# A hand-written order for attention with shared keys and values: a new sequence of steps, input loads one cycle earlier, and centred rows in PSUM at the end

## The chip, the cores and the metric

The kernel runs on one core of a Trainium2 chip. The metric is the device time of one execution in microseconds (us), lower is better. All arithmetic is float32. The engines are named as in the profile: PE multiplies matrices (PEld is its weight load), DVE, ACT and POOL work on vectors, SP issues the transfers (DMAs).

## What is computed

For 64 batches of x (128 tokens by 512), with 16 heads of size 64 that share one key and one value per token, the reference is:

```python
xn = layernorm(x, g_in)
q = (xn @ Wq).reshape(b, n, 16, 64).transpose(0, 2, 1, 3) * 64 ** -0.5
k, v = split(xn @ Wkv)                       # one head, shared by all 16
k = concat([null_k, k]); v = concat([null_v, v])   # one extra key ahead
sim = einsum('bhid,bjd->bhij', q, k) + bias  # bias of head, query, key
sim = where(causal_mask, -max, sim); sim = where(mask, sim, -max)
out = einsum('bhij,bjd->bhid', softmax(sim), v)
out = out.transpose(0, 2, 1, 3).reshape(b, n, 1024) @ Wo
return x + layernorm(out, g_out)
```

## The kernel before

**Tiling.** Batches are handled in pairs, and tokens in groups of four batches (GB = 4). The query product of a group is done by Strassen's scheme with sums of token blocks (xS1 to xS4, made on POOL at L492) and of weight blocks (wS): `q_one(c, k, h)` with k from 1 to 8 gives the products, named q1 to q8 below (a stroke, q1', marks the second half h = 1 of a cycle). A product is four matmuls (L597) of 256 columns into PSUM tiles pa, pc or pw. Three of the seven products are split once more, into leaves: `leaf(c, k, stage)`, called leaf(k,stage) here, multiplies sums of smaller blocks (xL2, xL3, xL4, made on POOL at L534, with one block of xT overwritten) at L553 into pl, and DVE adds the result to the query tile at L556. ACT copies pa out at L503 and L614 (L608 keeps a part, ku), DVE adds pc at L1001 and L1009 and L617.

The output product works likewise: `out_one(p, k)` (out1 to out7, eight matmuls each, L860), with sums of the attended values on POOL at L843 (`out_sum`), parts kept by ACT at L893 and added by DVE at L885.

**Softmax.** For each batch there are scores (PE, L651), added to bias and mask by DVE (L687), row maxima (DVE, L692), exps with row sums (ACT, L701), reciprocals (DVE, L718), the scaling by them (POOL, L722), a transpose of 32 by 32 blocks (DVE, L737), and the values (PE, L770). ACT evicts the values from PSUM at L810. The tile of bias plus mask is made on POOL (L635).

**Layer norms.** x is loaded (SP, L128, four DMAs per batch after the first groups), its statistics are taken on DVE (L284 to L288), the power on POOL (L289), and it is normed on ACT (L310), transposed in blocks on DVE (L331), written to DRAM (xd, L340) and read back as tokens (xT, L348). Keys and values come from xT (PE pkv, L358; DVE, L373); values go through DRAM too (vd, L387; vr, L399), keys are copied at L393. The output row y gets its statistics on DVE (L909 to L913), the power on POOL (L917), is normed on ACT (L932), multiplied by the gain (L953), added to the residual (L956) and stored (L960). The last batches do this on DVE alone: `pair_center` (L942) subtracts the mean and multiplies by the gain, `pair_scale` (L948) multiplies by the reciprocal deviation and adds the residual.

**Order.** No scheduler moves anything: each engine runs its instructions in the order in which the code emits them. The program is a front (a list of calls, with regions -1 and 0), then `cycle(c)` for c = 1 to 29, then a final list for the last six batches. Cycle c holds, for b0 = 2c and b1 = b0 + 1: the softmax of b0 and b1; the output product of p = b0 - 2 and p + 1; the output norm of r = b0 - 4 and r + 1; the norm of x for m = b0 + 10 and m + 1; the query products for b0 + 4. It ends with `region(c)`: the scores of b0 + 2 and b0 + 3 and the values of b0 and b0 + 1, which share the weights' half arrays. Even cycles begin a token group and so hold its POOL sums; odd cycles hold the tokens' read back. What sets the time of a step is thus its place in its engine's queue and the semaphores that it waits for; SP waits too, so a transfer stands behind the waits of those issued ahead of it. PSUM tiles come from small pools: pl, pw, pkv and pyw share two slots, pa and pc have one each, and the score tiles ("s") have one pool of their own. `nc.tensor.addr_align` pads PE's instructions so that a block of 256 begins at a chosen place.

Of the kernel before, what the change touches and what calls it, by code (L numbers as in the profile page):

```python
# [17 lines left out]
def kernel(  # L18
# [67 lines left out]
    GB = 4  # L86
# [847 lines left out]
    gain = [gob]  # L934

# [4 lines left out]
    def pair_center(b):  # L940
        mv, rstd = yn[b]
        nc.vector.scalar_tensor_tensor(  # L942
            ys[b], ys[b], mv[:, 0:1], gain[0], ALU.subtract, ALU.mult
        )

    def pair_scale(b):
        mv, rstd = yn.pop(b)
        nc.vector.scalar_tensor_tensor(  # L948
            ys[b], ys[b], rstd, res.pop(b), ALU.mult, ALU.add
        )  # L950
# [120 lines left out]
    def cycle(c):  # L1071
# [5 lines left out]
        fetch, send = (b0 + 5) // GB, (b0 + 7) // GB  # L1077
        if soft:
            scores_max(b1, 0)
        if first and LEAF <= c and more:  # L1080
            token_sum(c // 2 + 1, 1)
        if pair:
            values_out(p, (0, 2))
        if first and LEAF <= c and more:
            token_sum(c // 2 + 1, 3)
        if fin:
            pair_stats(r)
        if first and LEAF <= c and more:
            token_sum(c // 2 + 1, 2)
        if pair:  # L1090
            values_out(p + 1, (0, 2))
        if not first and fetch + 1 < NG:
            load_mask(fetch + 1)
        if m < B:
            load_x(m)
        if fin:
            pair_pow(r)
        if c == 1:
            tokens_in(2)
        if soft:  # L1100
            scores_max(b1, 1)
            scores_max(b0, 0)
        q_one(c, 1, 0)
        if fin:
            pair_stats(r + 1)
        if pair:
            values_out(p, (1, 3))
        if first and LEAF <= c and more:
            token_sum(c // 2 + 1, 4)
        if pair:  # L1110
            values_out(p + 1, (1, 3))
        if first and LEAF <= c and more:
            leaf_sums(c // 2 + 1, 2)
        if c < LEAF:
            q_one(c, 2, 0)
        if soft:
            exps(b0, 0, 0, 2)
            scores_max(b0, 1)
        if c >= LEAF:
            leaf(c, 2, 0)  # L1120
        q_one(c, 5, 0)
        q_one(c, 6, 0)
        if first and LEAF <= c and more:
            leaf_sums(c // 2 + 1, 3)
        if soft:
            exps(b0, 0, 2, 8)
        if pair:
            out_sum(p, 0)
        if first and LEAF <= c and more:
            leaf_sums(c // 2 + 1, 4)  # L1130
        out_one(p, 1)
        if pair:
            out_sum(p, 1)
        if fin:
            pair_pow(r + 1)
        if soft:
            rinv(b0, 0)
        q_one(c, 7, 0)
        if m + 1 < B:
            load_x(m + 1)  # L1140
        if c % 2 and n0 < B:
# [493 lines left out]
```

## Time and profile before

| quantity | value |
|---|---|
| median of 3 runs (lowest to highest) | 1035.18 us (1034.01 to 1036.33) |
| the profiled execution's own time | 1035.38 us |
| its span in the trace | 1033.6 us |
| granted PE clock | 0.997 |
| share of the span busy: PE, DVE, ACT, POOL | 98%, 84%, 62%, 76% |

A row of a timeline gives start, duration, engine, line, operation, output and input names, shapes and count, and in brackets how long the engine stood before it and what ended that. Durations of neighbouring rows overlap a little, since instructions are pipelined: the time from one start to the next says what a step costs its engine. A product of four matmuls takes PE 0.87 us from start to start, one of eight 1.73.

### The profile page before, as it was taken

The numbers are of one execution on the slowest core, as the hardware profiler recorded it, in microseconds if no ns is written. First come the engines' busy times: TensorE is split into PE (matmuls) and PEld (weight loads), VectorE is DVE, ScalarE is ACT, GpSimd is POOL, SyncE is SP. The second block draws the span as 40 slices with busy tenths as digits, with TensorE's granted clock in tenths as the row PEclk, the third lists the DMA queues.
The fourth block names the chain that finished last, engine by engine and source line by source line (L and its number), as shares of the span: only waits on it lengthen the run. The fifth ranks groups of instructions, "written<-read, shape, count | busy, mean of one in ns | idle before, by whom it ended". The sixth has DMA issues, their size and how long they took to land. (4 is left out here: it accounts for less than half of the span.)

```text
span 1033.6 us, 31778 instructions
## 1 busy us (share of the span) xinstructions
PE 1017.9 (98%) x12104; PEld 894.1 (87%) x12104; DVE 864.3 (84%) x2000; ACT 644.0 (62%) x2742; POOL 787.5 (76%) x710
## 2 busy tenths in 40 slices
PE   9999999999999999999999999999999999999996
PEld 8878888889888888888889888888888898888875
DVE  7766888888888898888888888888888988878898
ACT  2655776556775656766557765557756567755581
POOL 3699959588696877959679595886968779596774
PEclk9999999999999999999999999999999999999998
DMA  6541160522506144151521605225051431502202
GB/s 210 164 131 48 73 156 23 149 82 88 151 33 151 59 126 114 72 131 39 147 93 72 167 21 147 75 94 145 32 155 55 129 111 72 126 13 63 83 2 102
DMA packets 70263, 100.90 MB, mean 98 GB/s; under 512 B 27744, under 2 KB 31328, under 8 KB 68320
## 3 DMA queue, kind: packets, MB, share of 16 engines
q1 hardware_dynamic: 69008, 97.83, 33.3%
q8 instruction: 96, 1.57, 0.7%
q10 hardware_dynamic: 1104, 1.05, 0.3%
q14 instruction: 55, 0.45, 0.1%
HBM read 63.19 MB, written 33.55 MB: 94 GB/s over the span
## 5 line engine op out<-in xcount | busy, mean ns | idle before, releaser
L701 ACT ACTIVATE s<-s,nmax 128x65 f32<-128x65 f32 (+1 forms) x1024 | 377.0, 400 | 3.4 <-DVE nmax L692 3.4
L722 POOL TENSOR_TENSOR s<-s,rinv 128x1024 f32<-128x1024 f32 (+1 forms) x128 | 188.5, 1483 | 57.1 <-DVE rinv L718 56.6
L701 ACT ACTIVATION_READ_ACCUMULATOR s<-s,nmax 128x1 f32 x1024 | 229.2, 224 | 0.0
L635 POOL TENSOR_TENSOR s<-biasp,mneg 128x1552 f32<-128x1552 f32 x64 | 205.0, 3225 | 2.3 <-DMA x<-in_x_dram 2.0
L810 ACT ACTIVATE oT<-poX,nv 128x256 f32<-128x256 f32 x58 | 27.6, 476 | 219.8 <-PE poX L770 112.7
L556 DVE TENSOR_TENSOR qT<-pl,qT 128x128 f32<-128x128 f32 (+1 forms) x420 | 128.6, 329 | 9.5 <-PE pl L553 6.9
L687 DVE TENSOR_TENSOR s<-ps,s 128x256 f32<-128x256 f32 (+2 forms) x224 | 120.1, 604 | 15.7 <-PE ps L651 15.2
L860 PE MATMUL pyX<-wo,oT 128*128 128x256 f32 x512 | 121.5, 380 | 0.0
L692 DVE TENSOR_REDUCE nmax<-s 128x8 f32<-128x520 f32 (+1 forms) x128 | 118.8, 949 | 0.1
L860 PE MATMUL pyX<-wT,oT 128*128 128x256 f32 x488 | 115.5, 380 | 0.8 <-POOL oT L843 0.8
L737 DVE STREAM_TRANSPOSE sb<-s 128x1536 f32<-128x1536 f32 x64 | 112.9, 1764 | 0.2 <-POOL s L722 0.2
L860 PEld LDWEIGHTS pyX<-wo,oT 128*128 128x128 f32 x512 | 96.9, 190 | 14.6 <-issue 0.9
L860 PEld LDWEIGHTS pyX<-wT,oT 128*128 128x128 f32 x488 | 88.4, 190 | 10.8 <-POOL oT L843 1.2
L651 PE MATMUL ps<-kT,qT 64*64 64x128 f32 (+1 forms) x4096 | 93.6, 245 | 1.0 <-issue 1.0
L917 POOL TENSOR_TENSOR rstdo<-rstdo,nhalf 128x1 f32<-128x1 f32 x64 | 35.5, 557 | 75.6 <-PE pl L553 68.3
L651 PEld LDWEIGHTS ps<-kT,qT 64*64 64x64 f32 x4096 | 85.5, 134 | 6.0 <-issue 2.6
L289 POOL TENSOR_TENSOR rstd<-rstd,nhalf 128x1 f32<-128x1 f32 x64 | 37.3, 583 | 65.2 <-DVE rstd L288 59.2
L770 PE MATMUL pos<-sb,vr 32*64 32x128 f32 (+1 forms) x1792 | 81.8, 321 | 0.0
L770 PE MATMUL poY<-sb,vr 32*64 32x128 f32 x720 | 74.8, 347 | 0.2 <-issue 0.2
L770 PE MATMUL poX<-sb,vr 32*64 32x128 f32 x960 | 73.7, 299 | 0.0
L503 ACT COPY qT<-pa 128x256 f32<-128x256 f32 x168 | 66.7, 397 | 1.4 <-PE pa L597 1.4
L860 PE MATMUL pyw<-wo,oT 128*128 128x256 f32 x280 | 66.4, 380 | 0.3 <-POOL oT L843 0.2
(150 smaller groups left out, 2514.8 us busy)
## 6 DMA issues: line engine op xcount, KB each, us to landing
res<-in_x_dram SPq DMA_DIRECT2D x64, 256.0 KB, 3.0
out_dram<-y SPq DMA_DIRECT2D x58, 256.0 KB, 2.0
x<-in_x_dram SPq DMA_DIRECT2D x224, 64.0 KB, 2.7
xd<-xb SPq DMA_DIRECT2D x14, 1024.0 KB, 3.9
xT<-xd SPq DMA_DIRECT2D x56, 256.0 KB, 5.9
vr<-vd SPq DMA_DIRECT2D x64, 128.0 KB, 2.7
x<-in_x_dram SPq DMA_DIRECT2D x8, 256.0 KB, 4.9
vd<-vt SPq DMA_DIRECT2D x32, 64.0 KB, 2.2
```

The costliest lines, as they stand in the source:

```text
L289: nc.gpsimd.tensor_tensor(rstd, rstd, nhalf, ALU.pow)
L503: nc.scalar.copy(q_part(g, c, h), by_block("a"))
L556: nc.vector.tensor_tensor(o, p, o, ALU.add)
L635: nc.gpsimd.tensor_tensor(S[b], biasp, mneg[:, t].unsqueeze(1).broadcast_to([P, R8, ROW]), ALU.add,)
L651: nc.tensor.matmul(to[r][i * DH : (i + 1) * DH, f, :], qT[g, f // FH, t // GH][rows, f % FH, t % GH, NQ - 1 - i if hf else i], kT[g][rows, ...
L687: nc.vector.tensor_tensor(sv, ps, sv, ALU.add)
L692: nc.vector.tensor_reduce(nmax[b][:, hf], S[b][:, :, WITH_NULL[hf]], AX.X, ALU.max, negate=True)
L701: nc.scalar.activation(row, row, AF.Exp, bias=nmax[b][:, hf, k : k + 1], accum_out=rsum[b][:, hf, k : k + 1],)
L722: nc.gpsimd.tensor_tensor(sv, sv, rinvs.pop((b, hf)).unsqueeze(2).broadcast_to([P, R8, sv.shape[2]]), ALU.mult,)
L737: nc.vector.transpose(sb.rearrange("p j e q -> p e j q"), S[b][:, :, 1 : ROW - 1].rearrange("p e (j k) -> p e j k", k=Q),)
L770: nc.tensor.matmul(po[s][rows, half], vr[g][quad(s), j, t, :], sb[quad(s), slots, r * NF : (r + 1) * NF, :], start=start, stop=True, skip_ ...
L860: nc.tensor.matmul(prod[key], h[:, c, :], w[:, c, :], start=(start and c == 0), stop=(c == HC - 1), skip_group_check=not start,)
```

## The change

The work is the same but for one thing: in the last six batches `pair_center` writes the centred row to a PSUM tile, and `pair_scale` reads it there. All else is order:

- In `cycle`, nearly every call has a new place. q5 comes ahead of the leaf and of q6; q5' comes in the middle of the second half, right behind out6; leaf(2,3) and leaf(4,0) come earlier, q8' later. In cycle 1 (whose groups have no leaves) out2 stands between q7 and q4. The first norm of r has its statistics ahead of the maxima, xL3 and the first output sum come ahead of xS4 and xL2 on POOL.
- x is loaded a cycle ahead: cycle c loads m + 2 and m + 3, each behind a store, in place of m and m + 1 (cycle 1 loads all four).
- The front and the final list have new sequences.

The core of the diff:

```diff
@@ pair_center, pair_scale
+    y_mid = {}
     def pair_center(b):
         mv, rstd = yn[b]
+        if b < B - 6:
+            o = ys[b]
+        else:
+            if b // 2 not in yns:
+                yns[b // 2] = ps_s.tile([P, 2, DIM], FP, tag="s", name=f"yc_{b}")
+            o = y_mid[b] = yns[b // 2][:, b % 2]
         nc.vector.scalar_tensor_tensor(
-            ys[b], ys[b], mv[:, 0:1], gain[0], ALU.subtract, ALU.mult
+            o, ys[b], mv[:, 0:1], gain[0], ALU.subtract, ALU.mult
         )
     def pair_scale(b):
         mv, rstd = yn.pop(b)
         nc.vector.scalar_tensor_tensor(
-            ys[b], ys[b], rstd, res.pop(b), ALU.mult, ALU.add
+            ys[b], y_mid.pop(b, ys[b]), rstd, res.pop(b), ALU.mult, ALU.add
         )
@@ cycle
-        if m < B:
-            load_x(m)
...
-        if m + 1 < B:
-            load_x(m + 1)
...
+        if c == 1:
+            load_x(m)
...
+        if c == 1:
+            load_x(m + 1)
...
+        if m + 2 < B:
+            load_x(m + 2)
+        if soft:
+            nc.tensor.addr_align(256, offset={1: 120, B // 2 - 3: 76}.get(c, 94))
...
-        if soft:
-            nc.tensor.addr_align(256, offset={B // 2 - 3: 141}.get(c, 159))
...
+        if m + 3 < B:
+            load_x(m + 3)
+        if pair:
+            load_res(p + 1)
...
@@ front
-    q_one(0, 4, 0)
...
+    q_one(0, 4, 0)
+    q_one(0, 3, 0)
+    key_values(6)
+    q_one(0, 1, 1)
+    q_one(0, 2, 1)
+    q_half(2, 1)
...
@@ final list
     pair_center(B - 5)
     out_sum(B - 2, 1)
     out_sum(B - 2, 3)
+    pair_scale(B - 5)
     pair_pow(B - 3)
-    pair_center(B - 3)
     pair_scale(B - 6)
     store(B - 6)
-    pair_scale(B - 3)
-    store(B - 3)
-    pair_scale(B - 5)
+    out_one(B - 2, 5)
     store(B - 5)
     pair_pow(B - 4)
+    pair_center(B - 3)
+    pair_scale(B - 3)
     out_sum(B - 2, 2)
     pair_center(B - 4)
-    out_one(B - 2, 5)
+    stats_part(B - 2, 0)
     pair_scale(B - 4)
     store(B - 4)
     out_one(B - 2, 6)
     out_one(B - 2, 3)
-    stats_part(B - 2, 0)
     stats_part(B - 2, 1)
+    store(B - 3)
```

How the rows move on the engines:

**SP and POOL in the steady cycle.** SP's transfers from the end of an even cycle through the odd one behind it (x are the input rows, xd and xT the tokens, vd and vr the values, out_dram the stores), before:

```order
L340 DMA xd_7_4913<-xb_7_4433 128x2048
L387 DMA vd_6_4924<-vt_6_4922 512x1x32 x2
L348 DMA xT_7_4927<-xd_7_4913 32x4x512 x4
L138 DMA res_19_4934<-in_x_dram 128x512
L393 DMA kT_6_4389<-kT_6_4389 64x512
L145 DMA m8_7_5088<-in_mask_BxS_bk0_dram 128x512
L128 DMA x_32_5090<-in_x_dram 32x512 x4
L128 DMA x_33_5151<-in_x_dram 32x512 x4
L399 DMA vr_6_5193<-vd_6_4924 32x1024 x4
L960 DMA out_0_dram<-y_18_4753 128x512
L960 DMA out_0_dram<-y_19_4890 128x512
```

and now:

```order
L340 DMA xd_7_4932<-xb_7_4412 128x2048
L348 DMA xT_7_4936<-xd_7_4932 32x4x512 x4
L138 DMA res_18_4941<-in_x_dram 128x512
L387 DMA vd_6_4945<-vt_6_4943 512x1x32 x2
L393 DMA kT_6_4388<-kT_6_4388 64x512
L145 DMA m8_7_5084<-in_mask_BxS_bk0_dram 128x512
L399 DMA vr_6_5212<-vd_6_4945 32x1024 x4
L967 DMA out_0_dram<-y_18_4754 128x512
L128 DMA x_34_5264<-in_x_dram 32x512 x4
L967 DMA out_0_dram<-y_19_4892 128x512
L128 DMA x_35_5331<-in_x_dram 32x512 x4
```

The loads of x moved from ahead of vr to behind the two stores, and are those of the next cycle (34 and 35 for 32 and 33); vd moved behind xT. On POOL, the even cycle's sums before:

```order
L492 TENSOR_TENSOR xS4_7_5522<-xT_7_4927,xS2_7_5494 128x512
L534 TENSOR_TENSOR xL2_7_5526<-xT_7_4927 128x128 x2
L534 TENSOR_TENSOR xL2_7_5526<-xT_7_4927,xL2_7_5526 128x128
L534 TENSOR_TENSOR xT_7_4927<-xT_7_4927,xL2_7_5526 128x128
L534 TENSOR_TENSOR xL3_7_5544<-xT_7_4927 128x128 x2
L534 TENSOR_TENSOR xL3_7_5544<-xT_7_4927,xL3_7_5544 128x128 x2
L843 TENSOR_TENSOR yS_22_5555<-oT_23_5496 128x512
```

and now:

```order
L534 TENSOR_TENSOR xL3_7_5513<-xT_7_4936 128x128 x2
L534 TENSOR_TENSOR xL3_7_5513<-xT_7_4936,xL3_7_5513 128x128 x2
L843 TENSOR_TENSOR yS_22_5533<-oT_23_5507 128x512
L492 TENSOR_TENSOR xS4_7_5535<-xT_7_4936,xS2_7_5493 128x512
L534 TENSOR_TENSOR xL2_7_5537<-xT_7_4936 128x128 x2
L534 TENSOR_TENSOR xL2_7_5537<-xT_7_4936,xL2_7_5537 128x128
L534 TENSOR_TENSOR xT_7_4936<-xT_7_4936,xL2_7_5537 128x128
```

xL3 and the first output sum (yS) moved ahead of xS4 and xL2.

**PE in the front and in cycle 1.** The query products of the second group in the front (pq are products of the first group, pkv the keys and values), before:

```order
L597 MATMUL pc_1_0_5_662<-xT_1_377,wS_138 128x256 x2
L1406 ISA
L597 MATMUL pa_1_1_1_714<-xT_1_377,wq_81 128x256 x2
L597 MATMUL pw_1_1_2_719<-xT_1_377,wq_81 128x256 x2
L358 MATMUL pkv_6_732<-xT_1_377,wkv_84 128x256 x4
L597 MATMUL pa_1_1_1_714<-xS2_1_577,wS_138 128x256 x2
L1419 ISA
L597 MATMUL pc_1_1_5_745<-xS1_1_575,wS_138 128x256 x2
```

and now:

```order
L597 MATMUL pc_1_0_5_601<-xT_1_409,wS_138 128x256 x2
L358 MATMUL pkv_6_721<-xT_1_409,wkv_84 128x256 x4
L597 MATMUL pa_1_1_1_728<-xT_1_409,wq_81 128x256 x2
L1420 ISA
L597 MATMUL pw_1_1_2_734<-xT_1_409,wq_81 128x256 x2
L437 MATMUL pq_2_1_740<-xT_0_202,wq_81 128x256 x4
L1429 ISA
L597 MATMUL pa_1_1_1_728<-xS2_1_556,wS_138 128x256 x2
L597 MATMUL pc_1_1_5_764<-xS1_1_554,wS_138 128x256 x2
```

pkv moved between the first pc and the pa behind it, and pq_2 between the pw and the next pa. In cycle 1, q7, q4 and out2 before:

```order
L597 MATMUL pa_1_2_1_958<-xS2_1_577,wS_138 128x256 x2
L860 MATMUL pyX_0_1_990<-wo_91,oT_0_935 128x256 x4
L597 MATMUL pa_1_2_1_958<-xS3_1_467,wq_81 128x256 x2
L597 MATMUL pa_1_2_1_958<-xS4_1_580,wq_81 128x256 x2
L860 MATMUL pyw_0_2_1015<-wo_91,oT_0_935 128x256 x4
```

and now:

```order
L597 MATMUL pa_1_2_1_958<-xS2_1_556,wS_138 128x256 x2
L860 MATMUL pyX_0_1_990<-wo_91,oT_0_940 128x256 x4
L597 MATMUL pa_1_2_1_958<-xS3_1_538,wq_81 128x256 x2
L860 MATMUL pyw_0_2_1007<-wo_91,oT_0_940 128x256 x4
L597 MATMUL pa_1_2_1_958<-xS4_1_581,wq_81 128x256 x2
```

out2 (pyw) moved between the two products that use the same pa tile.

**DVE in the final list.** Centring and scaling of the batches B - 6 to B - 3, before:

```order
L942 SCALAR_TENSOR_TENSOR y_end_13023<-y_end_13023,mvo_13251,gain 128x512
L942 SCALAR_TENSOR_TENSOR y_end_13233<-y_end_13233,mvo_13382,gain 128x512
L948 SCALAR_TENSOR_TENSOR y_end_13023<-y_end_13023,rstdo_13247,res_13076 128x512
L948 SCALAR_TENSOR_TENSOR y_end_13233<-y_end_13233,rstdo_13384,res_12976 128x512
L948 SCALAR_TENSOR_TENSOR y_end_13023<-y_end_13023,rstdo_13253,res_13060 128x512
L942 SCALAR_TENSOR_TENSOR y_end_13233<-y_end_13233,mvo_13357,gain 128x512
L948 SCALAR_TENSOR_TENSOR y_end_13233<-y_end_13233,rstdo_13359,res_12960 128x512
L885 TENSOR_TENSOR y_end_13392<-pyY_5_13410,kyu_13421 128x256
```

and now (yc is the PSUM tile of the centred rows, stp the statistics of half a row):

```order
L949 SCALAR_TENSOR_TENSOR yc_13386<-y_end_13026,mvo_13251,gain 128x512
L955 SCALAR_TENSOR_TENSOR y_end_13026<-yc_13386,rstdo_13253,res_13061 128x512
L955 SCALAR_TENSOR_TENSOR y_end_13026<-yc_13386,rstdo_13247,res_13076 128x512
L949 SCALAR_TENSOR_TENSOR yc_13411<-y_end_13233,mvo_13382,gain 128x512
L955 SCALAR_TENSOR_TENSOR y_end_13233<-yc_13411,rstdo_13384,res_12947 128x512
L949 SCALAR_TENSOR_TENSOR yc_13411<-y_end_13233,mvo_13357,gain 128x512
L902 BN_STATS stp_13416<-y_end_13395 128x6
L955 SCALAR_TENSOR_TENSOR y_end_13233<-yc_13411,rstdo_13359,res_12962 128x512
```

Two scales moved ahead of the centring and scaling of B - 3 (y_end_13233 with mvo_13382), and half of the next batch's statistics ahead of the last scale.

377 lines of the change are left out of this document (183 added, 194 removed).

## The prediction

> **What bounds the kernel now.** I read the page first, then the waits, then a table of busy time cut at the first score product (L651) of some cycles, and last the timelines at the places where these cycles differ.
>
> ```profile
> span 1033.6 us, 31778 instructions
> PE 1017.9 (98%) x12104; PEld 894.1 (87%) x12104; DVE 864.3 (84%) x2000; ACT 644.0 (62%) x2742; POOL 787.5 (76%) x710
> ```
>
> PE is busy 98% of the span; no other engine comes near. So what can be won is what PE loses inside a cycle, plus the stretch at the end where another engine closes the program. The table of busy time (start and end, length, busy time of PE, PEld, DVE, ACT, POOL, clock, DMA) shows six late cycles and, last, two undisturbed ones:
>
> ```profile
> 190.93:222.55 31.62, 31.57 (x380) 27.46 (x379) 27.27 (x66) 20.19 (x86) 18.70 (x15) 1.00 0.56 137
> 377.92:409.57 31.65, 31.57 (x379) 27.46 (x378) 27.27 (x66) 20.20 (x86) 18.69 (x15) 1.00 0.54 136
> 440.86:472.08 31.22, 31.22 (x380) 27.55 (x379) 27.27 (x66) 20.21 (x86) 18.69 (x15) 1.00 0.56 138
> 503.18:535.19 32.01, 31.84 (x380) 27.39 (x379) 27.27 (x66) 20.20 (x86) 18.70 (x15) 1.00 0.55 134
> 628.44:661.03 32.59, 31.84 (x379) 27.39 (x379) 27.27 (x66) 20.19 (x86) 18.70 (x15) 1.00 0.54 132
> 754.26:785.84 31.58, 31.56 (x379) 27.47 (x379) 27.27 (x66) 20.20 (x86) 18.71 (x15) 1.00 0.52 136
> 816.94:847.98 31.04, 31.04 (x380) 27.63 (x379) 27.27 (x66) 20.29 (x86) 18.78 (x15) 1.00 0.54 139
> 847.98:879.07 31.09, 31.09 (x379) 27.62 (x378) 26.38 (x63) 20.17 (x86) 29.75 (x31) 1.00 0.17 62
> ```
>
> An undisturbed odd cycle takes 31.04 us, an even one 31.09, and PE has no gap in either. The six odd ones above exceed 31.04 by 0.58, 0.61, 0.18, 0.97, 1.55 and 0.54: **4.4 us**. The waits name what they have in common (us in total, times, longest):
>
> ```profile
> DVE st L284 <- DMA x<-in_x_dram: 9.4, 11, 2.0
> ...
> PEld pl L553 <- DVE qT L556: 6.4, 14, 1.0
> ```
>
> The worst cycle shows the chain, on SP, DVE and PE:
>
> ```profile
> 636.94 7.11 SPq L128 DMA_DIRECT2D x<-in_x_dram  x8
> ```
>
> ```profile
> 644.30 0.69 DVE L284 BATCH_NORM_STATS2 st<-x 128x6 f32<-128x512 f32 x1 [1.98 <-DMA x<-in_x_dram]
> ...
> 645.32 0.61 DVE L556 TENSOR_TENSOR qT<-pl,qT 128x256 f32<-128x256 f32 x2
> ```
>
> ```profile
> 644.37 1.03 PE L597 MATMUL pa<-xS,wS 128*128 128x256 f32 x4
> 645.98 0.49 PE L553 MATMUL pl<-xL,wq 128*128 128x128 f32 x2 [0.59 <-DVE qT L556]
> ```
>
> The eight x loads leave SP over 7.11 us; DVE reaches the statistics first and stands 1.98 us; the leaf sums (L556) queued behind are late; PE's next leaf product (L553) finds no free PSUM slot. Start to start PE needs 0.87 us for the four matmuls at 644.37 and took 1.61.
>
> **The steady cycle.** The order changes, the work doesn't: each product, eviction, sum, exp and scale stands once in both. The x loads of cycle c+1 are now issued in the second half of cycle c, each behind a store. A load that goes out some 20 us before use instead of 5 can wait for a store and still land first, against the longest stand of 1.98. So the 4.4 us go. The tokens' copy, its four loads and both residual loads remain on SP, and vd slips behind xT; its reader, the vr fetch of the next cycle, is wanted only by that cycle's region, so I charge nothing. If a store holds its x load too long, the stand comes back (below).
>
> What is late next I looked for by putting each moved step at its new place with the durations of the even cycle. The tightest that moved are on POOL:
>
> ```profile
> 858.17 0.88 POOL L534 TENSOR_TENSOR xL<-xT 128x128 f32<-128x128 f32 x2
> 859.00 1.00 POOL L534 TENSOR_TENSOR xL<-xT,xL 128x128 f32<-128x128 f32 x2
> 859.96 1.28 POOL L843 TENSOR_TENSOR yS<-oT 128x512 f32<-128x512 f32 x1
> ...
> 866.98 2.93 POOL L722 TENSOR_TENSOR s<-s,rinv 128x512 f32<-128x512 f32 x2
> 869.85 1.29 POOL L843 TENSOR_TENSOR oT<-oT,oT 128x512 f32<-128x512 f32 x1
> ```
>
> ```profile
> 868.60 0.69 DVE L956 TENSOR_TENSOR y<-yn,res 128x512 f32<-128x512 f32 x1
> ```
>
> ```profile
> 861.57 0.38 PE L553 MATMUL pl<-xT,wq 128*128 128x128 f32 x2
> ```
>
> ```profile
> 871.79 1.89 PE L860 MATMUL pyX<-wo,oT 128*128 128x256 f32 x8
> ```
>
> (The DVE row is the residual sum that the second store waits for.) xL2 and the xT made from it moved behind xL3 and the first output sum: 0.83, 0.96 and 1.22 start to start, less 0.3 that POOL stood before a pow whose statistics now come earlier. They were ready when xL3 began, at 858.2, and now at about 860.9; leaf(2,1) reads them at 861.57. Out of 3.4 us of slack 0.7 are left. The last output sum ended near 871.1 for out7 at 871.79; it stays behind the two scales and comes about 0.2 earlier, with 0.9 of slack. Nothing else that moved came under 0.5 in this walk, so I take the cycle at its old length. Its other PE losses, about 0.1 each at the first product and at region entry and 0.1 to 0.2 at q6, have the same predecessor on ACT before and after. The bounds: 0.06 us per cycle (the difference of the two undisturbed rows) either way over 28 cycles, 1.7 us; far worse only if a slack is gone (below).
>
> A second row decides whether the new alignment points are worth anything, in PEld of the third region:
>
> ```profile
> 100.43 0.13 PEld L770 LDWEIGHTS poY<-sb,vr 32*64 32x64 f32 x2 [0.47 <-issue]
> ```
>
> ```profile
> q8 instruction: 96, 1.57, 0.7%
> ```
>
> PE stood 0.47 us there for nothing the trace names; the undisturbed cycles have no room for such a stand. I price the moved points at 0, with a bound of 0.5 won here and as much lost at another place. The Trainium skill ("Runtime: NRT & Kernel Launch", section "Instruction fetch mechanics") says that instructions come in blocks of 16 KiB and that crossing into the next is mostly hidden; the queue's 96 packets with 1.57 MB agree with the block's size. By that rule moving the points gives 0 in every cycle, and by the row alone up to 0.47 in each; the undisturbed cycles above speak for the rule.
>
> **The front and cycle 1.** PE, start to start, loses here:
>
> ```profile
> 50.62 1.03 PE L597 MATMUL pc<-xT,wS 128*128 128x256 f32 x4
> 51.99 1.13 PE L597 MATMUL pa<-xT,wq 128*128 128x256 f32 x4 [0.35 <-ACT qT L614]
> ...
> 55.55 1.03 PE L597 MATMUL pa<-xS,wS 128*128 128x256 f32 x4
> 57.16 1.10 PE L597 MATMUL pc<-xS,wS 128*128 128x256 f32 x4 [0.58 <-DVE kT L373]
> ```
>
> ```profile
> 74.94 1.03 PE L597 MATMUL pa<-xS,wq 128*128 128x256 f32 x4
> 76.58 1.13 PE L597 MATMUL pa<-xS,wq 128*128 128x256 f32 x4 [0.61 <-ACT ku L608]
> ```
>
> 50.62 to 51.99 is 1.37 for a product of 0.87, so 0.50 is lost, and the one behind the wait takes 1.13 in place of 1.03; 55.55 to 57.16 loses 0.74, and 0.07 in the next. In the new front the keys product pkv (eight matmuls, 1.74) stands between the pc and the pa of the first, and four products stand between pkv and the pc of the second: **1.4 us** go. In cycle 1 out2, eight matmuls too, comes between the two pa's. 74.94 to 76.58 is 1.64; the 0.77 and the 0.10 behind it are covered: **0.9**. Nothing of it is won if the copies on ACT slide as far; and x9 and x8 now go out behind wo's load, so that DVE may stand for them: at the worst cycle's price 1.55, which would eat the front's gain. I take 1.4 and 0.9, since each cover is longer than its wait, and keep 0 as the bound.
>
> **The end.** DVE, with hardly a gap, closes the program; PE's last product is over near 1025.6.
>
> ```profile
> 1017.30 1.39 DVE L942 SCALAR_TENSOR_TENSOR y_end<-y_end,mvo,gain 128x512 f32<-128x512 f32 x2
> 1018.61 0.90 DVE L948 SCALAR_TENSOR_TENSOR y_end<-y_end,rstdo,res 128x512 f32<-128x512 f32 x1
> 1019.96 2.42 DVE L948 SCALAR_TENSOR_TENSOR y_end<-y_end,rstdo,res 128x512 f32<-128x512 f32 x2 [0.44 <-POOL rstdo L917]
> ...
> 1029.84 0.75 DVE L948 SCALAR_TENSOR_TENSOR y_end<-y_end,rstdo,res 128x512 f32<-128x512 f32 x1
> ```
>
> ```profile
> 1020.41 1.43 POOL L843 TENSOR_TENSOR oT<-oT 128x512 f32<-128x512 f32 x1
> ```
>
> ```profile
> 1023.72 1.89 PE L860 MATMUL pyw<-wT,oT 128*128 128x256 f32 x8
> ```
>
> With POOL idle one L948 takes 0.75; beside POOL's output sums it took 0.90, and two took 2.42. L942, which reads its gain from PSUM, took 1.39 for two beside the same sums. The centred rows in PSUM give L948 the operands of L942's kind, so I price it as that: 0.15 plus 0.92. The wait of 0.44 goes as two scales and a centring now stand ahead of the scale that needs that pow. Sum **1.5**; bounds 0.4 (PSUM does not help) and 1.5 (these are all its waits). PE's last product, over at 1025.6 and 4.2 before the last L948, comes no later than it did, so DVE should still close.
>
> **Sum.** 4.4 + 1.4 + 0.9 + 1.5 = 8.2. The profiled execution took 1035.38 us, 1.8 around its span, 0.2 above the median of the runs: 1035.4 - 8.2 = **1027.2 us**.
>
> **Rivals.** *Only the x waits go* (12%): copies slide with the new order in the front, and the end stays as it is. For it: ACT and DVE are rearranged at all these places. Then 1035.4 - 4.4 = 1031.0.
>
> *The x loads come no earlier* (5%): they stand behind stores, and a store waits for the residual sum on DVE. If that holds them until the next cycle's statistics, the waits stay: 1035.4 - 3.8 = 1031.6. Against it: the second residual sum ended at 869.3 of a cycle that ends at 879.07.
>
> *A small wait in each cycle* (9%): one of the slacks under 1 us is a little overdrawn. 0.1 to 0.3 us times 28 takes back 2.8 to 8.4: 1030.0 to 1035.6, within 0.2% in 4 of the 9.
>
> *A stand like that at 100.43 in every region* (1%): 0.47 times 29 is 13.6, 1040.8; against it, the undisturbed cycles.
>
> *Slower: out7 waits for POOL's last output sum* (12%). The sum stands behind the second scale, this behind a reciprocal on DVE, and that now behind both statistics of x. POOL, busy 29.75 of 31.09 us in even cycles, can't catch up there; odd ones have room (18.78). With 0.9 of slack and 14 even cycles it decides at 0.59 past the slack, 1.5 us late: 14 times 0.59 is the 8.2 won. At 1.0 past it, 1027.2 + 14 = 1041.2. For it: four of the POOL steps ahead were moved. Against it: in the walk the sum comes earlier, not later.
>
> **How the numbers follow.** Forecast 61%, between 1025.0 and 1029.5 by the bounds above. The range takes in the first two rivals and half of the third, and 1 us below for a stand that goes in the third region and a shorter steady cycle: 1024.0 to 1033.0. Two runs of this kernel can be told apart from about 0.2%, 2 us: faster 0.83 (61, 12, 5 and 5), same 0.04, slower 0.13.
>
> **What would show it.** All odd cycles at 31.04 and no wait of the x statistics for a DMA; no gap of PE over 0.3 at pa and pc in the front and at q4 of cycle 1; L955 at 0.7 each beside POOL, and DVE's last centring 1.5 us closer to PE's last product. Wrong would be cycles above 31.2 throughout, with PE waiting at leaf(2,1) for POOL or at out7; or the gap of 0.47 in every region.

## The result, and the profile after

The changed kernel takes **1027.26 us** (median of 4 runs, 1026.61 to 1028.00) where the kernel before took 1034.60 beside it (4 runs, 1033.10 to 1036.33): a ratio of 0.9929, with a 95% interval from 0.9910 to 0.9947. The forecast was 1027.2. The profiled execution took 1026.7 us for itself, 8.7 less than that of before. The head of its page:

```profile
span 1024.9 us, 31793 instructions
PE 1013.0 (99%) x12104; PEld 900.7 (88%) x12104; DVE 852.5 (83%) x2000; ACT 642.8 (63%) x2742; POOL 788.2 (77%) x710
```

PE has the same 12104 matmuls in a shorter span. The table of busy time, cut at the first score product (L651) of the same eight cycles as before (columns as in the prediction's table; the stretch called cycle c begins with the region that `cycle(c - 1)` ends with, and "the region of cycle c" is that one):

```profile
188.43:219.46 31.03, 31.03 (x379) 27.82 (x378) 27.20 (x66) 20.16 (x86) 19.37 (x15) 1.00 0.49 123
374.81:405.85 31.04, 31.04 (x380) 27.82 (x379) 27.22 (x66) 20.18 (x86) 19.37 (x15) 1.00 0.45 122
436.94:467.97 31.03, 31.03 (x379) 27.82 (x378) 27.20 (x66) 20.17 (x86) 19.37 (x15) 1.00 0.46 122
499.07:530.10 31.03, 31.03 (x380) 27.81 (x379) 27.21 (x66) 20.19 (x86) 19.33 (x15) 1.00 0.45 123
623.32:654.35 31.03, 31.03 (x379) 27.80 (x378) 27.21 (x66) 20.18 (x86) 19.34 (x15) 1.00 0.49 122
747.58:778.61 31.03, 31.03 (x380) 27.82 (x379) 27.21 (x66) 20.18 (x86) 19.35 (x15) 1.00 0.46 122
809.71:841.01 31.30, 31.30 (x379) 27.97 (x378) 27.47 (x66) 20.16 (x86) 19.36 (x15) 1.00 0.46 122
841.01:872.11 31.10, 31.10 (x380) 27.82 (x379) 25.67 (x63) 20.17 (x86) 29.33 (x31) 1.00 0.16 62
```

The six late cycles are at 31.03 or 31.04 like the other odd ones, and the even ones are unchanged. (The seventh row is long by 0.27; the last section says why.) The wait that made them late is all but gone, and no leaf product waits for DVE's leaf sums (L556) any more. The row of the waits on x, and on SP, DVE and PE the place that cost 1.98 us before:

```profile
DVE st L284 <- DMA x<-in_x_dram: 0.6, 2, 0.4
```

```profile
622.51 3.07 SPq L348 DMA_DIRECT2D xT<-xd  x4
...
626.16 1.24 SPq L387 DMA_DIRECT2D vd<-vt  x2
...
641.84 1.82 SPq L128 DMA_DIRECT2D x<-in_x_dram  x4
```

```profile
637.11 0.68 DVE L284 BATCH_NORM_STATS2 st<-x 128x6 f32<-128x512 f32 x1
...
638.12 0.61 DVE L556 TENSOR_TENSOR qT<-pl,qT 128x256 f32<-128x256 f32 x2
```

The statistics (no bracket: no wait) and the leaf sums run on, and the x loads that go out at 641.84 are those of the next cycle. By cuts at the same places of both traces, the 8.7 us come from here:

| stretch | before | after | difference | forecast |
|---|---|---|---|---|
| six odd cycles, over 31.04 | 4.43 | -0.06 | -4.5 | -4.4 |
| cycle 0 (front, up to cycle 1's scores) | 30.50 | 29.84 | -0.7 | -1.4 |
| cycle 1 | 32.34 | 31.41 | -0.9 | -0.9 |
| from the end of the last region (cycle 30) on | 53.60 | 52.42 | -1.2 | -1.5 |
| regions of cycles 2, 4, 12 and 25, over 5.29 | 1.10 | 0.52 | -0.6 | 0 |
| region of cycle 30 | 8.72 | 8.16 | -0.6 | 0 |
| start of the first region, all else | | | -0.3 | 0 |

The regions (scores and values, L651 and L770) differ from one execution to the next: a second execution of the changed kernel (experiment 10) has 5.53 in cycle 2, 5.45 in cycle 3, 5.29 in cycle 25 and 8.99 in cycle 30. So the -1.2 in the two rows of regions is not the change's to keep, and the medians, 7.3 apart, say about what the other rows sum up to.

PE in the front and in cycle 1:

```profile
49.62 1.03 PE L597 MATMUL pa<-xS,wq 128*128 128x256 f32 x4
51.31 1.10 PE L597 MATMUL pc<-xT,wS 128*128 128x256 f32 x4 [0.67 <-issue]
52.25 1.89 PE L358 MATMUL pkv<-xT,wkv 128*128 128x256 f32 x8
```

```profile
74.14 1.03 PE L597 MATMUL pa<-xS,wq 128*128 128x256 f32 x4
75.01 1.89 PE L860 MATMUL pyw<-wo,oT 128*128 128x256 f32 x8
76.73 1.03 PE L597 MATMUL pa<-xS,wq 128*128 128x256 f32 x4
```

Cycle 1 went as forecast: 74.14, 75.01 and 76.73 follow without a gap. In the front the two old stands are gone, but a new one has come ahead of the pc at 51.31: from 49.62 it is 1.69 for a product of 0.87, so 0.82 is lost, and 0.07 more on the slowed pc. "Issue" means that no semaphore held it. What stood in the stream is shown by the rows of line 1408, the new padding in front of this product (count, shortest, median and longest duration in ns, first and last start):

```profile
L1408 PEldq NOP  x30: 13/13/13, 49.1 to 51.2; - x30
```

Thirty no-operations in 2.1 us, one every 71 ns, directly ahead of the pc. The four matmuls in front of it keep PE busy for 0.87 us only. Before the change a padding of the same size (L1397) stood behind a product of eight, and cost nothing: the eight began at 48.03 and the next product at 49.76.

The end, on DVE, POOL and PE:

```profile
1009.75 0.74 DVE L949 SCALAR_TENSOR_TENSOR yc<-y_end,mvo,gain 128x512 f32<-128x512 f32 x1
1010.53 1.41 DVE L955 SCALAR_TENSOR_TENSOR y_end<-yc,rstdo,res 128x512 f32<-128x512 f32 x2
...
1012.82 0.75 DVE L955 SCALAR_TENSOR_TENSOR y_end<-yc,rstdo,res 128x512 f32<-128x512 f32 x1
...
1021.10 0.75 DVE L955 SCALAR_TENSOR_TENSOR y_end<-yc,rstdo,res 128x512 f32<-128x512 f32 x1
```

```profile
1010.13 1.27 POOL L843 TENSOR_TENSOR oT<-oT 128x512 f32<-128x512 f32 x1
...
1012.39 1.28 POOL L843 TENSOR_TENSOR oT<-oT 128x512 f32<-128x512 f32 x1
```

```profile
1016.04 1.89 PE L860 MATMUL pyw<-wT,oT 128*128 128x256 f32 x8
```

Beside POOL's output sums the scale L955 of the last six batches now takes 0.70 to 0.75, as long as alone. The last one starts 5.06 us behind the start of PE's last product, where it was 6.12 before.

### The profile page after: what moved, and what is told of

Its sections match the earlier page's. It is cut to its first block, busy times and chain, and to the rows that moved or that the text cites. A ratio compares the mean times of both kernels' runs of the same rounds, so it can differ in the third digit from the quotient of the medians.

```text
span 1024.9 us, 31793 instructions
## 1 busy us (share of the span) xinstructions
PE 1013.0 (99%) x12104; PEld 900.7 (88%) x12104; DVE 852.5 (83%) x2000; ACT 642.8 (63%) x2742; POOL 788.2 (77%) x710
## 5 line engine op out<-in xcount | busy, mean ns | idle before, releaser
L701 ACT ACTIVATE s<-s,nmax 128x65 f32<-128x65 f32 (+1 forms) x1024 | 382.2, 413 | 3.5 <-DVE nmax L692 3.5
L701 ACT ACTIVATION_READ_ACCUMULATOR s<-s,nmax 128x1 f32 x1024 | 242.0, 236 | 0.0
L556 DVE TENSOR_TENSOR qT<-pl,qT 128x128 f32<-128x128 f32 (+1 forms) x420 | 122.4, 323 | 3.3 <-PE pl L553 3.3
L692 DVE TENSOR_REDUCE nmax<-s 128x8 f32<-128x520 f32 (+1 forms) x128 | 116.5, 949 | 0.1
L651 PE MATMUL ps<-kT,qT 64*64 64x128 f32 (+1 forms) x4096 | 93.7, 246 | 0.4 <-issue 0.4
L651 PEld LDWEIGHTS ps<-kT,qT 64*64 64x64 f32 x4096 | 85.5, 134 | 5.5 <-issue 2.1
L770 PE MATMUL pos<-sb,vr 32*64 32x128 f32 (+1 forms) x1792 | 81.4, 321 | 0.0
L843 POOL TENSOR_TENSOR yS<-oT 128x512 f32<-128x512 f32 x32 | 40.8, 1274 | 45.4 <-ACT oT L810 42.0
L770 PE MATMUL poY<-sb,vr 32*64 32x128 f32 x720 | 74.6, 348 | 0.0
L770 PE MATMUL poX<-sb,vr 32*64 32x128 f32 x960 | 73.5, 299 | 0.0
L331 DVE STREAM_TRANSPOSE xb<-x 128x512 f32<-128x512 f32 x56 | 39.4, 705 | 34.1 <-ACT x L310 34.1
```

The costliest lines, as they stand in the source:

```text
L556: nc.vector.tensor_tensor(o, p, o, ALU.add)
L651: nc.tensor.matmul(to[r][i * DH : (i + 1) * DH, f, :], qT[g, f // FH, t // GH][rows, f % FH, t % GH, NQ - 1 - i if hf else i], kT[g][rows, ...
L692: nc.vector.tensor_reduce(nmax[b][:, hf], S[b][:, :, WITH_NULL[hf]], AX.X, ALU.max, negate=True)
L701: nc.scalar.activation(row, row, AF.Exp, bias=nmax[b][:, hf, k : k + 1], accum_out=rsum[b][:, hf, k : k + 1],)
L770: nc.tensor.matmul(po[s][rows, half], vr[g][quad(s), j, t, :], sb[quad(s), slots, r * NF : (r + 1) * NF, :], start=start, stop=True, skip_ ...
L843: nc.gpsimd.tensor_tensor(o, l, m, op)
```

## Experiments

Three sets of kernels were run, each on one chip beside the kernel before. Experiments 1 and 4 to 8 have a single run, so one time and one trace. In all these traces the first region starts between 33.7 and 35.1 us, the region of cycle 2 takes 5.5 to 6.0 and the last one 8.2 to 9.1, whatever the edit; so I read a single run in the stretch that its edit touches, not in its total.

**1. The changed kernel with the old load times of x (a_x_late).** Which edit took the 4.4 us?

```diff
@@ cycle (first half; the same for m + 1)
-        if c == 1:
+        if m < B:
             load_x(m)
@@ cycle (second half; the same for m + 3)
-        if m + 2 < B:
-            load_x(m + 2)
```

> The changed kernel with its loads of x put back to where they were: cycle c loads m and m + 1 at its start, the rest of the new order stays. Theory (the loads' lateness alone made the long odd cycles): the waits of the x statistics for a DMA come back, six to eight odd cycles are 0.2 to 1.6 us over 31.03 again, in sum 4 to 5 us, span near 1029.4. Rival (the new order of the cycle, which changed DVE's queue, took the waits away): odd cycles stay at 31.03 and the span at 1024.9.

It took 1029.81 us, and my theory fell in the cuts that matter: the six late cycles stay away (odd cycles are 31.03 or 31.04 but for 3, 15 and 17, whose regions are 0.15 to 0.50 long), and the x statistics wait once, for 1.3 us at the start. SP in the cycle that was the worst:

```profile
624.79 2.58 SPq L348 DMA_DIRECT2D xT<-xd  x4
...
627.95 1.25 SPq L387 DMA_DIRECT2D vd<-vt  x2
...
630.59 5.70 SPq L128 DMA_DIRECT2D x<-in_x_dram  x8
```

In a cycle that begins at 625.89 the x loads leave 4.7 us into it, where they left 8.5 us into it before, and the statistics come at 639.69 without a wait. The loads are as late in the order as ever; what stands ahead of them has become shorter. Over the changed kernel's trace it loses 1.3 at the first region's start (35.06) and the rest in regions (5.44 to 5.97 in cycles 2, 3, 15 and 17, and 9.01 in cycle 30).

**2. The kernel before with the x loads early (b_x_early).** The other way round:

```diff
@@ cycle
-        if m < B:
+        if c == 1:
             load_x(m)
@@ behind store(r); m + 3 likewise behind store(r + 1)
+        if m + 2 < B:
+            load_x(m + 2)
```

> The kernel before with one edit: the loads of m + 2 and m + 3 go out behind the two stores of cycle c, and cycle 1 loads all four. Theory: the long odd cycles fall to 31.04, 4.4 us less, near 1030.5 where the kernel before has 1034.9; everything else stays. Rival (the old order has no room for the loads behind the stores, and they come late or hold the residual loads up): under 2 us less, with new waits of DVE for a DMA.

1030.48 us (1029.91 to 1030.79), ratio 0.9960 (0.9948 to 0.9973); all odd cycles 31.03 or 31.04, one x wait of 0.9 left. Loading early is enough by itself, too.

**3. The kernel before with vd behind xT (b_vd_behind).** What in the new order was it, then? In before, SP's waits name the transfer of the values, and the changed kernel's name the write of the tokens instead (total, times, longest):

```profile
SPq L387 <- DVE qT L556: 84.3, 14, 10.2
```

```profile
SPq L348 <- DMA xd<-xb: 51.1, 14, 4.4
```

vd waits up to 10.2 us for DVE, 84.3 in all, and SP issues nothing meanwhile: xT, the residual, the keys, the mask and the eight x loads all stand behind it.

```diff
@@ cycle, ahead of region(c)
-        if first and send < NG:
-            values_send(send)
         if first and toks:
             tokens_in(m // GB)
+        if first and send < NG:
+            values_send(send)
```

> The kernel before with one edit: at the end of an even cycle the four loads of the tokens (xT) are issued ahead of the two stores of the values (vd), as in the changed kernel; the loads of x stay where they were. The run with the x loads put back had no long odd cycles, and there SP issued xT at 624.8 where the kernel before issued it at 630.9, behind vd, which waits for a DVE transpose that ends the cycle. Theory (SP's queue: xT and so x stood behind that wait): the long odd cycles fall to 31.04, 4.4 us less. Rival (the place of the statistics and of the other steps on DVE took the waits away): they stay long, 0 to 1 us less.

1030.50 us (1030.46 to 1031.02), ratio 0.9948 (0.9929 to 0.9967), all odd cycles 31.03 or 31.04, one x wait of 0.8 left. In the cycle that was the worst SP now issues xT from 624.69 and the x loads from 630.86, where it issued them from 630.91 and 636.94 before. **Swapping two issues takes the whole 4.4 us**, with every x load at its old place. The two edits cure the same wait; their gains don't add up.

**4. The changed kernel with the centred rows in SBUF (a_sbuf_rows).**

```diff
@@ pair_center
-        if b < B - 6:
-            o = ys[b]
-        else:
-            if b // 2 not in yns:
-                yns[b // 2] = ps_s.tile([P, 2, DIM], FP, tag="s", name=f"yc_{b}")
-            o = y_mid[b] = yns[b // 2][:, b % 2]
+        o = ys[b]
```

> The changed kernel with the centred rows of the last batches kept in SBUF, in place, as before; the new order of the final list stays. Theory (a scale with both operands in SBUF is held up by POOL's sums): the three scales that lie beside POOL's output sums take 0.9 to 1.5 us in place of 0.7, 1.0 to 1.5 us in sum, and DVE's last instruction ends that much later. Rival (the gain at the end is the order's alone): the scales stay at 0.75 and the end where it is.

1028.87 us. DVE's scales (here L950) and the POOL sum beside the second of these rows:

```profile
1011.61 2.10 DVE L950 SCALAR_TENSOR_TENSOR y_end<-y_end,rstdo,res 128x512 f32<-128x512 f32 x2
...
1014.45 1.44 DVE L950 SCALAR_TENSOR_TENSOR y_end<-y_end,rstdo,res 128x512 f32<-128x512 f32 x1
```

```profile
1014.08 1.27 POOL L843 TENSOR_TENSOR oT<-oT 128x512 f32<-128x512 f32 x1
```

From the first centring of this stretch to the last scale it takes 12.46 (1010.83 to 1023.29) against 11.35 in the changed kernel (1009.75 to 1021.10): the PSUM rows are worth **1.11 us**. The scale at 1014.45 ends at 1015.89, 0.54 behind POOL's end at 1015.35, as if it had begun only then.

**5. The changed kernel with out2 behind q4 in cycle 1 (a_out2_late).**

```diff
@@ cycle, between q7 and q4
-        out_one(p, 2)
+        if c >= LEAF:
+            out_one(p, 2)
...
         if c < LEAF:
             q_one(c, 4, 0)
+            out_one(p, 2)
```

> The changed kernel with out2 of cycle 1 behind q4 again, as before. Theory: q4 waits for ACT's copy of the product ahead of it in the same PSUM tile, and cycle 1 takes 32.3 in place of 31.41. Rival (ACT's new order in that cycle is what covers it): 31.4 to 31.6.

1029.20 us; cycle 1 takes 32.28 in place of 31.41, **0.87** as forecast, and the old stand is back:

```profile
75.82 1.13 PE L597 MATMUL pa<-xS,wq 128*128 128x256 f32 x4 [0.61 <-ACT ku L608]
```

**6. More work on POOL, first try (a_pool_more).** Where does POOL's lateness start to cost, the mechanism of my slower rival?

```diff
@@ cycle, behind token_sum(c // 2 + 1, 4)
+            nc.gpsimd.tensor_tensor(
+                xS[g3, 3],
+                xT[g3][:, GB // 2 :][:, :, hi_k],
+                xT[g3][:, GB // 2 :][:, :, lo_k],
+                ALU.subtract,
+            )
```

> The changed kernel with one more POOL sum of 512 columns (1.24 us, xS3 made a second time) ahead of xL2 in each of the 14 even cycles that hold token sums. Measures the slack that the new order leaves at leaf(2,1): the trace has xT ready at 854.16 and read at 854.60. Theory (slack 0.44): PE waits 0.8 and loses 0.1 behind it, even cycles 31.9 to 32.0, 12 us more in sum. If the slack is the 0.7 that the prediction worked out: 0.5 to 0.6 a cycle, 8 us. Rival (POOL's waits take it up): nothing.

1068.77 us, and it tells nothing on the question: xS3 made a second time makes q7 wait for it.

```profile
PE pa L597 <- POOL xS L1121: 33.3, 14, 2.9
```

**7. More work on POOL, second try (a_pool_more2).** Three sums of 128 columns, into a tile whose real sums come later, so that nobody waits for them:

```diff
@@ cycle, behind token_sum(c // 2 + 1, 4)
+            b11, b12, b21, b22 = leaf_tokens(c // 2 + 1, 3)
+            for _ in range(3):
+                nc.gpsimd.tensor_tensor(xL[c // 2 + 1, 3][:, 2], b22, b12, ALU.subtract)
```

> The changed kernel with three more sums of 128 columns on POOL (0.41 us each, one block of xL3 made again, read only much later) ahead of xL2 in each of the 14 even cycles with token sums. The extra sum of the run before was one that q7 reads, so PE waited for it directly; this one measures the slack at leaf(2,1): xT ready at 854.16, read at 854.60. Theory (slack 0.44): PE waits 0.8 and loses 0.1 behind it, even cycles 31.9 to 32.0 in place of 31.09, 12 us in sum. If the slack is 0.7: 0.5 to 0.6 a cycle. Rival (taken up elsewhere): 31.1.

1053.88 us. The even cycles answer the question; POOL and PE in cycle 4 at leaf(2,1), and the two waits:

```profile
171.03 1.53 POOL L1122 TENSOR_TENSOR xL<-xT 128x128 f32<-128x128 f32 x3
...
173.34 0.46 POOL L534 TENSOR_TENSOR xL<-xT,xL 128x128 f32<-128x128 f32 x1
173.88 0.45 POOL L534 TENSOR_TENSOR xT<-xT,xL 128x128 f32<-128x128 f32 x1
```

```profile
173.29 0.38 PE L553 MATMUL pl<-xT,wq 128*128 128x128 f32 x2
173.85 0.71 PE L553 MATMUL pl<-xL,wL 128*128 128x128 f32 x4 [0.18 <-POOL xL L534]
```

```profile
PE pos L770 <- issue: 9.4, 11, 1.5
PE pl L553 <- POOL xL L534: 2.8, 14, 0.5
PE pyX L860 <- POOL oT L843: 2.8, 14, 0.7
```

The extra sums delay POOL by 1.48 us. PE loses 0.35 and 0.10 at leaf(2,1) and 0.32 and 0.10 at out7: each even cycle from 4 to 26 is 31.95 to 31.98, 0.87 longer; without its region cycle 2 is 1.2 longer, and cycle 28 is 0.44 longer, which makes 12.1 us in the 14 of them. That is the total I had expected, but by luck: I had put all of it at leaf(2,1), and half of it arose at out7. But the time rose by 27, and the first of the three waits shows the other half: eleven stands of up to 1.5 us in the values' matmuls, for "issue". They lie in odd cycles, whose regions take up to 7.18 us in place of 5.29 (13.9 us over all of them), though no work was added there.

**8. The same with xT's loads behind the values' store (a_more2_vd).** Beside the stands lay a transfer that I had not looked at: a 16 KB packet of the instruction queue. In the changed kernel's undisturbed regions it starts between 0.3 us before the first score product and 0.5 behind it; in the regions of 6.3 us and more here it came 1.4 to 2.2 behind it. xT's loads go out just ahead of it: in cycle 5 SP issues them from 190.12 to 191.89, and the packet starts at 193.85. The edit moves them away:

```diff
@@ cycle, ahead of region(c)
-        if first and toks:
-            tokens_in(m // GB)
         if pair:
             load_res(p)
         if first and send < NG:
             values_send(send)
+        if first and toks:
+            tokens_in(m // GB)
+        if first and send < NG:
             keys_send(send)
```

> The kernel with three extra 128-column GpSimd sums a pair of cycles (1053.88 us, odd regions up to 7.18 us where 5.29 is the undisturbed length), with one more edit: the loads of xT are issued behind the values' store and read-back, not ahead of it. Theory A (a late fetch of TensorE's instructions: in that kernel the 16 KB packet of the instruction queue was recorded 1.3 to 2.1 us behind the start of each of the odd regions of 6.3 us and more, and from 0.5 us before to 0.3 us behind it for nearly all those of 5.29; it comes behind the loads of xT, which in the changed kernel begin later relative to the region): with xT's loads out of its way the packet comes about the region's start again, odd regions 5.29 to 5.5, odd cycles 31.03 to 31.3, total about 1040 (1053.9 less some 14). Theory B (the odd regions are long for a reason on GpSimd or VectorE, such as the late sum of scores): regions stay at 6 to 7.2 and the total at 1052 to 1055. Either way the even cycles stay at about 31.96.

**1039.38 us**: every odd region is 5.29 and every odd cycle 31.03 or 31.04, while the even ones from 4 to 26 stay at 31.95 to 31.99. POOL and DVE have the same work in both kernels; only the transfers' order differs. In the view of the transfers, 0.2 us about the packet of cycle 5 (193.77 in the first kernel, whose region began at 191.67; 190.31 in the second, whose began at 190.71):

```profile
q1 hardware_dynamic: 29, 0.04, 91.4%
q8 instruction: 1, 0.02, 31.7%
```

```profile
q8 instruction: 1, 0.02, 29.5%
```

In the first it comes amid 29 others, 2.1 us into the region; in the second it is the only packet on the core's queues. Its own time is about the same: 31.7% of 16 engines times 0.2 us is 1.01 us, and 29.5% is 0.94. It wasn't slow, it was late.

**9. Three more edits at once (a_best).** The padding ahead of q4, so that the product of eight covers it; in cycle 29 q5' ahead of q6, which covers a stand of 0.47 there; and batch B - 8 ("item 28" below) normed over ACT and a PSUM tile, since its two steps on DVE stood beside POOL for 1.70 and 1.88:

```diff
@@ front
+    nc.tensor.addr_align(256, offset=32)
     q_one(0, 4, 0)
...
-    nc.tensor.addr_align(256, offset=40)
     q_one(0, 3, 0)
@@ cycle
+        if c == B // 2 - 3:
+            q_one(c, 5, 1)
         q_one(c, 6, 1)
...
-        q_one(c, 5, 1)
+        if c != B // 2 - 3:
+            q_one(c, 5, 1)
@@ final list
+    pair_nmr(B - 8)
     exps(B - 1, 1, 0, 8)
-    pair_center(B - 8)
+    pair_norm(B - 8)
...
-    pair_scale(B - 8)
+    pair_gain(B - 8)
+    pair_residual(B - 8)
```

> The changed kernel with three more edits where its trace still shows losses. (1) The 30 padding instructions ahead of q3 in the front go ahead of q4, behind a product of eight matmuls: at 71 ns each they take 2.1 us of PE's instruction stream, and PE lost 0.9 at 51.3. (2) In the last cycle q5' stands between leaf(2,1) and q6', whose PSUM tile waits 0.6 for ACT. (3) Batch B - 8 is normed on ACT into PSUM and multiplied and added by DVE from there, in place of centring and scaling in SBUF, which took 1.70 and 1.88 beside POOL. Theory: 0.9 + 0.7 + 1.0 to 1.9, 1023.7 to 1024.7 where the changed kernel has 1027.3. Rivals: without the padding's place PE stands at another point of the front; the end is set by POOL's scaling of the last batch and not by DVE, and (3) gives nothing: then 1025.7.

1029.78 us (1028.29 to 1030.61), ratio 0.9939 (0.9921 to 0.9957): no better than the changed kernel. Up to the scores of the last cut it led by 1.67 (962.61 against 964.28); cycle 0 took 28.94 and cycle 29 took 29.44, as expected. Then the third edit made a new wait on PE, and 2.42 us of one on DVE behind it:

```profile
998.65 0.32 PE L770 MATMUL pos<-sb,vr 32*64 32x128 f32 x2 [2.70 <-DVE y L963]
```

The normed row sits in a slot of the score pool, which the values need; PE waits until DVE has read it. The two slow steps went, and a tile's lifetime took more than they had cost.

**10. The first two of these alone (a_best2), beside the changed kernel once more (after_again).**

> The changed kernel with two more edits: the padding of 30 no-operations moved from ahead of query product q3 of cycle 0 to ahead of q4, and q5 of cycle 29 moved ahead of q6. The two were seen to take 0.90 us from the front and 0.60 us from cycle 29 in the trace of the kernel that also changed the normalization of item 28; that third edit is dropped here. Theory (losses of the TensorE add along its own chain): front 28.94 instead of 29.84, cycle 29 29.44 instead of 30.04, the end as in the changed kernel (47.1 us from the last region but one's cycle on), in all -1.5 us: 0.9985 of the changed kernel's median on the same chip, with a profiled span of about 1023.4. Rival (cycle 29's saving is given back at the end, because VectorE's chain and not TensorE's sets it): -0.9 us, about 1026.3 where the changed kernel has 1027.2.

> The changed kernel itself, unaltered, on the same chip as its improved version, so that the two are compared directly. Every theory: 1026.5 to 1028.5 us, cycles 31.03 and 31.09.

1026.14 us (1025.28 to 1026.67, 6 runs) against **1027.58** (1026.55 to 1028.03, 6 runs) for the changed kernel on the same chip: 0.9986 of it. Against the kernel before the ratios are 0.9933 (0.9919 to 0.9948) and 0.9946 (0.9933 to 0.9959). Cycle 0 took 28.94 for 29.84 and cycle 29 took 29.44 for 30.05, 1.5 in sum, and 1.4 of it reached the median; one of the changed kernel's six times (1026.55) lies under the highest of the other's. PE in the front:

```profile
49.76 1.03 PE L597 MATMUL pa<-xS,wq 128*128 128x256 f32 x4
50.62 1.03 PE L597 MATMUL pc<-xT,wS 128*128 128x256 f32 x4
51.49 1.89 PE L358 MATMUL pkv<-xT,wkv 128*128 128x256 f32 x8
```

The same products without the stand: the padding was the cause of it. This is the lowest median of the kernels run here.

## Why the prediction was right, point by point

The mechanism of the terms held in the main, and the time lies in the range; that it came within 0.1 us of the forecast is luck. The forecast takes 8.2 from the profiled execution of the kernel before (1035.38), while the medians lie 7.3 apart (1034.60 and 1027.26), and the front and the end together gave 1.0 less than their terms.

- **The x waits (4.4).** Right in size (4.5), and too narrow in cause. I gave the gain to the earlier loads and wrote that vd "slips behind xT", for which "I charge nothing". Experiments 1 to 3 show that this slip alone removes the waits, and the early loads alone do too. I had priced vd by who reads it, not by who stands behind it on SP while it waits. The total didn't suffer, because both edits were made.
- **The front (1.4).** The term that was mis-sized: 0.7. Both old stands went, the first (0.50 and 0.10) as forecast. The second (0.74 and 0.07, the pc at 57.16) I had misread. The profile puts it down to DVE's kT, but the trace records kT's signal at 57.136, when that pc's weight load had already begun (57.132); the loads that a signal did release at 51.99 and 645.98 began 41 ns behind it. What stood ahead of the pc is a padding of 25 no-operations, behind a product of four:

```profile
L1419 PEldq NOP  x25: 13/13/13, 55.4 to 57.1; - x25
```

  The last of them starts at 57.094, 38 ns ahead of the load; in the new stand the times are 51.239 and 51.278. By these times 0.8 of the 1.4 was a cost of padding, not a wait, and it went because the padding of 25 there (now ahead of q6') stands behind a product of eight; no run moves that padding alone. The new stand is of the same kind: I had costed the moved alignment points at 0 in every place, and one set 30 no-operations ahead of the pc behind a product of 0.87 us. That takes 0.9 back (rows at 49.62 and 51.31, confirmed by experiment 10). The bound of 0.5 for these points was too small.
- **Cycle 1 (0.9).** Right: 0.9 in the cut, and 0.87 when out2 is put back.
- **The end (1.5).** Too large by 0.3. The PSUM rows give 1.11 (experiment 4), which is the term of 0.15 + 0.92. The pow's wait of 0.44 went too, but most of it was lost again: behind the last region 1.2 us are gone, and the close on DVE came 1.06 nearer to PE's last product (6.12 to 5.06), where I had named 1.5 as the sign. The rows of DVE say what took 0.3 back. From 1009.75 to 1017.01 (1017.30 to 1025.75 before) the four scales take 2.88 us from start to start for 4.36, so the 1.5 of the forecast is there. But two of the three centrings now stand directly ahead of the scale that reads them (0.78 and 0.85, where two in a row took 0.65 each), and the three cost 0.15 more in all; the last addition now stands right ahead of the statistics that read it and costs 0.12 more (0.46 for 0.34). I had priced this order as free.
- **The steady cycle (0).** Right: 31.03 and 31.09 for 31.04 and 31.09. The slacks behind it were read from the wrong row in one case. POOL and PE of an even cycle in the changed kernel:

```profile
853.16 0.46 POOL L534 TENSOR_TENSOR xL<-xT,xL 128x128 f32<-128x128 f32 x1
...
862.79 1.28 POOL L843 TENSOR_TENSOR oT<-oT,oT 128x512 f32<-128x512 f32 x1
```

```profile
854.82 0.61 PE L553 MATMUL pl<-xL,wL 128*128 128x128 f32 x4
...
864.83 1.89 PE L860 MATMUL pyX<-wo,oT 128*128 128x256 f32 x8
```

  At leaf(2,1) I measured up to its first pair of matmuls and the overwritten block of xT, and estimated 0.7. In experiment 7 that pair started at 173.29 without waiting, though the block was ready only at 174.33: it doesn't read it. What waits are the four matmuls behind it, which read xL2: ready at 853.62 for 854.82, a slack of 1.2. POOL's delay of 1.48 less 1.2 is 0.28, and 0.35 was measured. At out7 the last output sum ends at 864.07 for 864.83: 0.76 where I said 0.9. The delay of 1.48, less 0.45 that PE had lost already, less 0.76, is 0.27; 0.32 was measured.
- **The slower rival** (out7 waits for POOL) didn't occur, but its price was of the right kind: in experiment 7, with 0.3 past the slack, out7 waited in 14 cycles and cost 0.4 in the one shown.
- **The regions** gave -1.2 in the profiled execution, where the prediction had 0 with a bound of 0.5; they vary from one execution to the next, see below. Without them the terms sum to 7.6 of the 8.2 forecast.

## What to carry to other kernels

Price a moved DMA issue by what stands behind it on its queue while it waits for a semaphore, not only by its reader: here a store that waited for DVE held eight loads, and swapping it with the next issue was worth as much as loading a cycle ahead. When two edits cure one wait, undo each alone before giving either the gain. Padding and instruction fetch are part of the schedule: put padding behind a long product, and compare a wait's signal with the start of what it is said to release, since padding can end at the same moment. When an engine stands for "issue", look for the instruction queue's packet and for the transfers around it.

## What the hardware showed that I had not expected

**A late instruction packet stops PE.** For each region I took the packet's start from the transfers cut into stretches of 0.05 us, its duration from its share, and so its landing relative to the first score product, in us (good to about 0.05):

```text
kernel           cycle  landing  region       kernel          cycle  landing  region
before           17     1.07     5.29         a_pool_more2    17     1.31     5.29
before            4     1.65     5.56         a_pool_more2    21     1.69     5.54
before            2     2.24     5.93         a_pool_more2    19     2.37     6.13
changed          24     1.44     5.29         a_pool_more2     7     2.40     6.30
changed          25     1.61     5.57         a_pool_more2     9     3.01     6.85
changed           2     1.89     5.53         a_pool_more2     5     3.19     7.11
```

In these kernels and that of experiment 8, all regions of cycles 2 to 29 whose packet lands by 1.45 us are 5.29 or 5.30 long, and behind that point the region grows by as much as the landing is late, within 0.3 (two of before, landing at 1.63 and 1.67, grow by 0.02 at most). The traces of the other nine runs agree: of all 364 regions of cycles 2 to 29, 323 have their packet by 1.45 us and take 5.29 to 5.35, and the other 41 grow by as much as it is late, within 0.35. This covers the differences between regions that I had called stands of no known cause: cycles 2, 4 and 12 of before, cycles 2 and 25 of the changed kernel. (The longer region of cycle 30 I have not fitted.) That the transfers beside the packet set its landing is shown for the odd cycles of experiment 7, by experiment 8; why it is late in cycle 2 of every trace wasn't tried.

The Trainium skill ("Runtime: NRT & Kernel Launch", section "Instruction fetch mechanics") calls the crossing into the next block mostly hidden. That agrees with the steady cycles of the changed kernel; experiment 7 differs from it, with up to 1.89 us exposed in a region and 13.9 in all.

**Padding costs issue time.** 30 no-operations took PE's sequencer 2.1 us, 71 ns each, though each shows a duration of 13 ns. Behind a product of eight (1.73 us) 30 of them cost nothing; behind one of four (0.87) 30 cost 0.82, and 25 cost 0.74 in the kernel before.

**DVE waits for the whole of POOL's instruction.** With both operands in SBUF a scale that starts beside a POOL sum ends 0.54 us behind the sum's end (1015.89 and 1015.35 in experiment 4), and with the centred row in PSUM it takes its normal 0.75. The same 0.54 is in the prediction's rows of 0.90 and 2.42: their scales end at 1019.51 and 1022.38, and POOL's sums at 1018.97 and 1021.84. The Trainium skill ("SBUF — State Buffer", section "SBUF: two separate sides") says that a DVE operation with two SBUF inputs and a GpSimd operation that reads SBUF lock a shared pair of ports against each other for the whole instruction. The rows agree: the scale waits with two inputs in SBUF, and not with one of them in PSUM.
